# A two-layer cross-attention kernel: layer 0's context laid out with image rows first for every second entry, one value product shared by two entries, five semantic products for six, and a rewritten end

## The chip, the cores and the metric

The kernel runs on one core of a Trainium2 chip. The metric is the device time of one execution in microseconds (us); where several runs are given, their median counts. TensorE is called PE below (PEld is its weight load), VectorE DVE, ScalarE ACT, GpSimd POOL, and SP is the engine whose queue issues most of the DMAs.

## The reference, cut to what matters

Two cross-attention layers follow each other over 16 entries. An entry has 256 queries of 320 channels and a context of 256 rows of 512 channels; there are 20 heads of 16 channels. Layer 0 takes the first 77 context rows as text and the other 179 as image rows:

```python
q, k_text, v_text = hidden @ Wq, text @ Wk, text @ Wv
probs = softmax(q_h @ k_h.T * scale)                     # 77 text keys, by head
text_out = probs @ v_h
ip_k, ip_v = ip @ Wk_ip, ip @ Wv_ip                      # 179 image keys
scores = q_h @ ip_k_h.T * scale
text_probs = softmax(q @ k_text.T * scale)               # over all channels, not by head
sem = ((text_probs @ text) @ ip.T) * scale               # "semantic" scores, one for all heads
ip_probs = softmax(scores + 0.5 * sem) * spatial_mask
out = (text_out + ip_probs @ ip_v_h) @ Wout + bout + hidden
```

Layer 1 takes all but the last four context rows as text and the last four as image rows, normalises the attended text by its length for its semantic scores, and is otherwise alike. Only its last steps are touched by the change.

## The kernel before, in words

**Precision.** A float32 number is held as a high and a low part in the PE's rounded format, and a product of two such numbers is three matmuls (high by high, high by low, low by high): `prod`, L240. `halves` makes the two parts: ACT copies the high part (L165) and DVE or POOL subtracts it for the low part (L168). A product's third block of 64 output channels holds two terms in one matmul's 128 columns (`prod_m`, L250), which `evacuate` adds up (L259 to L262).

**Slots.** The work is written as 80 slots for layer 0 and 80 for layer 1. Slot k of layer 0 stands for one group of four heads of one entry, so five slots are an entry and ten a pair of entries. `slot0` writes, in this order: the maxima of group k+1 (`maxima0`, L753, a transpose whose result a DMA of ACT's queue puts into the stack of queries), half of the scores of k+2 (`score0`, L745; DVE takes their maxima in L746 and L747), half of the scores of k with keys on the partitions (`turned0`, L769; ACT takes the exponential in L772 and POOL multiplies by the semantic factor `rs` in L775), the attended values of k-1 (`attend0`, L804), the other halves, and the DMAs of the stacks of k+4 (`stacks0`). Between these, `fill` places whatever task is due: a table at the end gives each task's steps their slots, shifted by ten for each pair c. The PE's order is the written one; a scheduler orders DVE, ACT and SP; POOL's queue is worked in its order.

**Stacks.** For each group a stack `ks` of keys holds 48 key rows, 77 rows of the semantic factors M (the text part of them zero) and two rows that pick a maximum; `qs` is its partner. Keys and queries reach the stacks through DRAM (`kd`, `qd`). There are four stacks of each. In `score0` the keys are the moving operand, in `turned0` they are the weights, cut into two tiles of 128 rows.

**Values of layer 0.** The context of a pair lies in four tiles (`cta`, `ctb`), text first and image rows behind it. The values of an entry are made by `values0_` in three products of 128 context rows: rows 0 to 127 by the text weights (`wC`), rows 0 to 127 by the image weights (`wD`) and rows 128 to 255 by `wD`. ACT writes each to `vr`, scaled by a mask of rows. A pair so takes six products of twelve matmuls, 128x320 each. `attend0` takes for every head the three parts in turn. Column 16 of each head in `vr` holds the mask, written once at the start by `marks` (L334).

**Semantic scores.** `tokens0` makes M from the text rows and the image rows (77 columns of weights, 192 moving; POOL clears M's text part, L435). `semantic0` multiplies queries by text keys in six matmuls for each half (L667): three blocks of channels, high and low parts of the queries, each by the 156 columns of `kt`, which holds high and low parts of the keys. POOL copies the keys to `kt` (L385).

**The start.** `begin` is ordered by hand. SP issues loads and small DMAs back to back, among them the rows of `ks` that pick a maximum (`fields`, `ks<-mt`).

**The end.** Slots 158 and 159 hold the last groups of layer 1, slot 160 what is left of them. `attend1` adds to the values of k (L954) a product for k-1 (L964) whose operand DVE finishes in L943 from a PE product (L942) and POOL's rest (L933). Behind slot 160 the entry before the last is closed (`close1`: L1073, `split`, project L610 and L613, DVE L850, `out_dram<-xc`), and then the last one (`close_last`): its residual is loaded to `xc`, and it ends in L1121 with the product of the image probabilities by `output_values`, a matrix prepared in L1092 to L1105.

## Time and profile before

| what | value |
|---|---|
| three runs | 1497.43 us median (1495.08 to 1497.73) |
| the profiled execution's own time | 1499.52 us |
| its span (first to last instruction) | 1497.7 us |
| granted PE clock, mean | 0.984 |
| PE, POOL, DVE, ACT busy | 95%, 81%, 78%, 59% |
| PE in the chain that ended last | 73% of the span |

A row of the windows view gives, for a stretch of the span, each engine's busy time with its instructions, the granted PE clock, the share of time in which the DMA engines were busy, and GB/s. A row of a timeline gives start, duration, engine, line, operation, operands, shapes and count, and in brackets how long the engine was idle before it and on what. A row of groups ends in total and mean duration and the idle time before them. A row "X" of the chain gives start, duration and what the time was spent on. Line numbers are those of the kernel before; the rows of order of the kernel after have its own.

### The profile page before, as it was taken

To read this page: it belongs to the slowest core of one execution; us is meant where nothing else is said; L and a number is where in the kernel's file an instruction comes from. 1 tells how busy PE (TensorE), PEld (TensorE's weight loads), DVE (VectorE), ACT (ScalarE), POOL (GpSimd) and SP (SyncE) were. 2 spreads that over 40 slices of the span, in tenths; PEclk is the share of its full clock that TensorE was granted. 3 is DMA by queue.
4 is the path that set the end of the run, shared out by engine and by line. 5 is a ranking of instruction groups with operands and counts; after the bars stand their busy time and mean duration, and the time that the engine had idled before them with its cause. 6 is when DMAs were issued, how large, how long until landed. Compare 5 with 4: busy or idle time off the path is not lost.

```text
span 1497.7 us, 36123 instructions
## 1 busy us (share of the span) xinstructions
PE 1427.8 (95%) x12740; PEld 1155.6 (77%) x12740; DVE 1170.2 (78%) x2593; ACT 884.8 (59%) x1975; POOL 1215.2 (81%) x1304
## 2 busy tenths in 40 slices
PE   8789999999999899789999999999999999999997
PEld 8678888888888778577777777777777777777765
DVE  5467777777777787878887788778877887788785
ACT  5346565656565555556666666666666666666562
POOL 4259797979797977887698879887988798879786
PEclk9799999999999999999999999999999999999999
DMA  7767787778787776775434434443444344433411
GB/s 237 201 185 217 201 228 200 217 206 224 199 231 193 219 200 173 186 216 150 145 102 132 127 108 128 127 127 108 127 128 127 109 126 129 127 108 103 122 26 39
DMA packets 230986, 234.32 MB, mean 156 GB/s; under 512 B 39127, under 2 KB 200678, under 8 KB 230790
## 3 DMA queue, kind: packets, MB, share of 16 engines
q1 hardware_dynamic: 228598, 230.71, 55.4%
q8 instruction: 102, 1.67, 0.5%
q10 hardware_dynamic: 2208, 1.30, 0.4%
q14 instruction: 78, 0.64, 0.1%
HBM read 118.04 MB, written 77.04 MB: 130 GB/s over the span
## 4 chain that ended last, share of the span: by engine, by line
PE 73%; DVE 8%; DMA 6%; POOL 6%; issue 3%; ACT 3%; SPq 1%; ACTq 0%; DVEq 0%; POOLq 0%
PE X L942 15%; PE X L240 14%; PE P L804 6%; PE X L610 5%; PE P L954 5%; PE S L745 5%; PE P L964 4%; PE T L769 4%; PE T L894 3%; PE S L900 3%; PE X L613 2%; PE X L250 2%; PE X L579 2%; POOL P L775 2%; DVE mn L747 1%
## 5 line engine op out<-in xcount | busy, mean ns | idle before, releaser
L775 POOL TENSOR_TENSOR P<-P,rs 128x512 f32<-128x512 f32 x320 | 414.4, 1318 | 90.2 <-ACT P L772 89.3
L933 POOL TENSOR_TENSOR wt<-P,ctb 128x512 f32<-128x512 f32 x320 | 410.6, 1308 | 72.8 <-ACT ctb L932 72.8
L942 PE MATMUL X<-ctb,gm 128*128 128x512 f32 x1120 | 305.4, 402 | 5.8 <-DVE wt L943 5.7
L772 ACT ACTIVATE P<-T 128x512 f32<-128x512 f32 x320 | 175.4, 594 | 159.5 <-PE T L769 101.9
L943 DVE TENSOR_TENSOR wt<-X,wt 128x512 f32<-128x512 f32 x320 | 216.1, 680 | 42.7 <-PE X L942 36.4
L942 PEld LDWEIGHTS X<-ctb,gm 128*128 128x128 f32 x1120 | 195.3, 188 | 39.0 <-DVE wt L943 8.7
L914 ACT ACTIVATE P<-T 128x512 f32<-128x512 f32 x320 | 173.0, 593 | 76.2 <-PE T L894 73.3
L932 ACT ACTIVATE ctb<-P 128x512 fp32r<-128x512 f32 x320 | 186.7, 627 | 36.8 <-PE X L942 33.1
L902 DVE TENSOR_REDUCE mn<-S 128x4 fp32r<-128x1008 f32 x160 | 191.3, 1196 | 0.0
L747 DVE TENSOR_REDUCE mn<-S 128x4 fp32r<-128x716 f32 x160 | 142.2, 889 | 0.0
L804 PE MATMUL P<-P,vr 128*32 128x256 f32 x1920 | 127.4, 396 | 5.3 <-DVE tmp L821 2.0
L745 PE MATMUL S<-ks,qs 125*128 125x256 f32 x640 | 117.7, 307 | 4.9 <-DMA ks<-M 2.8
L745 PEld LDWEIGHTS S<-ks,qs 125*128 125x128 f32 x640 | 89.0, 195 | 40.1 <-issue 20.9
L1031 POOL TENSOR_TENSOR r<-u,rs 128x40 f32<-128x40 f32 (+2 forms) x17 | 108.7, 6394 | 3.9 <-DVE u L1028 3.9
L769 PE MATMUL T<-qs,ks 127*128 127x256 f32 x640 | 108.2, 292 | 0.4 <-DMA qs<-mt 0.4
L746 DVE TENSOR_REDUCE mn<-S 128x4 fp32r<-128x308 f32 x160 | 74.4, 465 | 31.2 <-PE S L745 30.8
L815 DVE STREAM_TRANSPOSE nt<-P 128x512 f32<-128x512 f32 x80 | 56.9, 711 | 51.8 <-PE P L804 51.3
L769 PEld LDWEIGHTS T<-qs,ks 127*128 127x128 f32 x640 | 92.1, 198 | 2.0 <-DMA qs<-mt 1.0
L804 PEld LDWEIGHTS P<-P,vr 128*32 128x32 f32 x1920 | 57.2, 112 | 47.0 <-issue 8.1
L954 PE MATMUL P<-P,v1t 128*32 128x256 f32 x1280 | 85.7, 385 | 0.0
L964 PE MATMUL P<-wt,zone 128*32 128x256 f32 x1280 | 85.1, 381 | 0.3 <-DVE wt L943 0.3
L610 PE MATMUL X<-ho,wF 128*128 128x256 f32 x512 | 74.3, 287 | 6.5 <-ACT mt L755 4.0
(297 smaller groups left out, 2974.5 us busy)
## 6 DMA issues: line engine op xcount, KB each, us to landing
qd<-q SPq DMA_DIRECT2D x96, 256.0 KB
qs<-tph SPq DMA_DIRECT2D x64, 320.0 KB
rawc<-in_cT_dram SPq DMA_DIRECT2D x60, 256.0 KB
qs<-qd SPq DMA_DIRECT2D x80, 192.0 KB
ks<-kd SPq DMA_DIRECT2D x80, 192.0 KB
ks<-kd SPq DMA_DIRECT2D x160, 96.0 KB
qs<-qd SPq DMA_DIRECT2D x160, 96.0 KB
kd<-kst SPq DMA_DIRECT2D x57, 256.0 KB
```

Of the source, the lines that this page charges most:

```text
L240: last = mm(out, lhs(a, k), rhs(b, k), start=i == 0, stop=i == len(terms) - 1)
L745: mm(sp[:, h], Q[: XROW + T0, h, t * 128 : (t + 1) * 128], K[: XROW + T0, h], start=True, stop=True)
L769: mm(st[p][:, j], K[:KS0, 2 * p + j, t * 128 : (t + 1) * 128], Q[:KS0, 2 * p + j], start=True, stop=True)
L772: exp = anchor(nc.scalar.activation(pt, st[p], AF.Exp, scale=SCALE))
L775: anchor(nc.gpsimd.tensor_mul(pt, pt, rs[:, t : t + 1].to_broadcast([128, 2, S])))
L804: mm(pv[32 * s : 32 * s + 32, o : o + S], v[:, vt, h : h + 32], P[k, s // 2][:, t, s % 2], start=vt < 2, stop=vt != 1,)
L902: anchor(nc.vector.tensor_reduce(maxes[k + 2][:, t], sp[:, :, :T1], axis=AX.X, op=ALU.max))
L914: anchor(nc.scalar.activation(P[k, u][:, t], st[u], AF.Exp, scale=SCALE))
L932: nc.scalar.activation(R[k, u][:, t], P[k, u][:, t], AF.Copy, scale=0.5)
L933: anchor(nc.gpsimd.tensor_sub(W[k, u][:, t], P[k, u][:, t], f(R[k, u][:, t])))
L942: mm(yp, gm[:, gb], R[k, u][:, kt], start=i == 0, stop=i == len(blocks[n]) - 1)
L943: nc.vector.tensor_mul(W[k, u][:, n], yp, W[k, u][:, n])
```

## The change

**Layout.** Context tiles get 51 zero columns ahead and are laid out, for each half, as text of both entries (2 x 77), image rows of the even entry (179), 26 zeros, image rows of the odd entry (179) and one more column. Cuts of 128 columns out of this are: 51 zeros and the even entry's text; the odd entry's text; and one that holds 51 image rows of the even entry, zeros and 51 of the odd one. Even entries now have image rows first (179) and text last, odd ones text first.

**Values.** `values0_` makes two products for an entry and a new task `vm` one for both: five products for a pair. `mark` writes the mask columns at each entry, and `attend0` takes the parts of even entries in another order.

```diff
-    def values0_(b):
-        for t, (w,), lo, sc in ((0, wv0, 0, tmask[:, 0:1]), (1, wvi0, 0, tmask[:, 1:2]), (2, wvi0, 128, 1.0)):
+    def value_rows(ct, at, w, *to):
+        vp = bank()[:, :320]
+        prod(vp, lambda s, k: side(ct[k], s, at, 128), lambda s, k: w(s, k), 4)
+        for V, t, sc in to:
+    def values0_(b):
+        ct, i = ct0[b // 2], b % 2
+        V = mark(b)
+        value_rows(ct, T0 if i else -MIX, wv0[0], (V, 0, masks(b)[0]))
+        yield
+        value_rows(ct, CI + (CG + MIX if i else 0), wvi0[0], (V, 2, 1.0))
+    def values_mixed(c):
+        to = [(vr[(b + 2) % 3], 1, masks(b)[1]) for b in (2 * c, 2 * c + 1)]
+        value_rows(ct0[c], CI + 128, wvi0[0], *to)
+    def mark(b):
+        V = vr[(b + 2) % 3]
+        for t, m in enumerate(masks(b)):
+            nc.gpsimd.tensor_copy(vcols(V, V0W)[:, t, :, 16], m.to_broadcast([128, H]))
...
-        task(("v0", 2 * c), shifted(n, -7, -5.4, -5), lambda b=2 * c: values0_(b), *k)
-        task(("v0", 2 * c + 1), shifted(n, -4, -3.8, -3.4), lambda b=2 * c + 1: values0_(b), *k)
+        task(("v0", 2 * c), shifted(n, -7, -5.4), lambda b=2 * c: values0_(b), *k)
+        task(("vm", c), shifted(n, -4.2), lambda c=c: values_mixed(c), *k)
+        task(("v0", 2 * c + 1), shifted(n, -3.8, -3.4), lambda b=2 * c + 1: values0_(b), ("vm", c))
```

The first place is the PE between the attended values of groups 43 and 44, in a pair in the middle of layer 0 (`wD` and `cta`, `ctb` are the image weights and the context, `vr` the values, `P` the probabilities). Before:

```order
L769 MATMUL T<-qs_95,ks_99 128x256 x4
L240 MATMUL X<-wD,cta_81 128x320 x3
L240 MATMUL X<-wD,cta_82 128x320 x3
L240 MATMUL X<-wD,ctb_83 128x320 x3
L240 MATMUL X<-wD,ctb_84 128x320 x3
L240 MATMUL X<-wD,cta_81 128x320 x3
L240 MATMUL X<-wD,cta_82 128x320 x3
L240 MATMUL X<-wD,ctb_83 128x320 x3
L240 MATMUL X<-wD,ctb_84 128x320 x3
L753 MATMUL X<-ident_r,mn_566 8x128 x2
```

The same place after (L252 is L240 before, L862 is L769, L846 is L753):

```order
L862 MATMUL T<-qs_95,ks_99 128x256 x4
L252 MATMUL X<-wD,cta_81 128x320 x3
L252 MATMUL X<-wD,cta_82 128x320 x3
L252 MATMUL X<-wD,ctb_83 128x320 x3
L252 MATMUL X<-wD,ctb_84 128x320 x3
L846 MATMUL X<-ident_r,mn_613 8x128 x2
```

One of two products of twelve matmuls is gone there; the other products of a pair stay in their slots, two of them in exchanged order.

**Copies that come in pieces.** The halves of the context and the evacuation of image keys are written in two pieces, text and image, or one for each entry. Key texts are 154 columns wide, not 156, and the copies to `kt` are 154 wide; the third block of keys is also copied to partitions 64 to 127.

```diff
             if i:
-                halves(*ahead.pop(0), eng, wait)
+                hi, lo, src = ahead.pop(0)
+                if isinstance(hi, list):
+                    for piece in zip(hi, lo, by_side(src)):
+                        halves(*piece, eng, "pieces")
...
-                    nc.gpsimd.tensor_copy(kt[:n, m, :, :, :T0], f(kst[:n, :, :, :T0]))
+                    for h in range(2):
+                        for p in range(0, 128, n):
+                            nc.gpsimd.tensor_copy(kt[p : p + n, m, h, :, :T0], f(texts(kst)[:n, h]))
```

The second place is POOL, in a pair in the middle of layer 0, from a group's last copy of attended values on (`hsn`). `cta` and `ctb` are the context's low parts, `P` the probabilities times `rs`. Before:

```order
L824 COPY hsn<-hsn 128x8x16
L435 MEMSET M_260 77x2x77
L775 TENSOR_TENSOR P_120<-P_120,rs_115 128x512
L775 TENSOR_TENSOR P_121<-P_121,rs_115 128x512
L168 TENSOR_TENSOR cta_81<-rawc_118,cta_81 128x512
L822 TENSOR_TENSOR hsn<-tmp_808 128x8x16
L168 TENSOR_TENSOR cta_82<-rawc_117,cta_82 128x512
```

After, where L868 is L775, L175 is L168 and L919 is L822:

```order
L868 TENSOR_TENSOR P_121<-P_121,rs_116 128x512
L868 TENSOR_TENSOR P_122<-P_122,rs_116 128x512
L175 TENSOR_TENSOR cta_81<-rawc_119,cta_81 128x154
L175 TENSOR_TENSOR cta_81<-rawc_119,cta_81 128x2x179
L175 TENSOR_TENSOR cta_82<-rawc_118,cta_82 128x154
L175 TENSOR_TENSOR cta_82<-rawc_118,cta_82 128x2x179
L919 TENSOR_TENSOR hsn<-tmp_848 128x8x16
```

The copy of `hsn` and the clearing of M are gone from POOL's queue, and each subtraction of 512 columns has become two.

**Semantic scores, M and the stacks.** The low parts of the third block of queries lie on partitions 64 to 127 of the same tile, so five matmuls do for six. M's zeros are written once at the start, at both ends of a wider tile. The stacks `ks` are 77 columns wider; even entries use them from column 77 on (`turned_ks`), and `fields` issues one more small DMA for each of the four.

```diff
-            for k in range(3):
-                qt = lambda h: qh[:, h, k, t * 128 : (t + 1) * 128]
-                for h in range(2):
-                    mm(sf[:, : 2 * NT].rearrange("p (s n) -> p s n", s=2), qt(h), kt[:, k], start=k + h == 0, stop=k + h == 3)
+            for k, h in ((0, 0), (0, 1), (1, 0), (1, 1), (2, 0)):
+                qt = qh[:, h, k, t * 128 : (t + 1) * 128]
+                mm(sf[:, : 2 * NT].rearrange("p (s n) -> p s n", s=2), qt, kt[:, k], start=k + h == 0, stop=k == 2)
...
-        Q, K = QK[k] = qs[k % SIZES["NR"]], ks[k % SIZES["NR"]]
+        Q, K = QK[k] = qs[k % SIZES["NR"]], (ks if b % 2 else turned_ks)[k % SIZES["NR"]]
...
             dma(ks[i][XROW + T0 : KS0, :, :T0], ind0r[:2, :T0].unsqueeze(1).to_broadcast([2, 4, T0]))
+            dma(ksw[i][XROW + T0 : KS0, 4 * S :], ind0r[:2, :T0])
```

**An entry's last group.** The sum of attended values is written by DVE to both places at once, in layer 0 (POOL's addition and copy, L822 and L824, go) and in layer 1 (POOL's copy L1014 goes).

```diff
-        nc.gpsimd.tensor_add(hn[:, g // 2, :, g % 2], tmp[:, 0], tmp[:, 1])
         if g == NG - 1:
-            nc.gpsimd.tensor_copy(hn[:, 2, :, 1], hn[:, 2, :, 0])
+            nc.vector.tensor_add(hn[:, 2], *[tmp[:, i].unsqueeze(2).to_broadcast([128, 8, 2, 16]) for i in range(2)])
             later(0.45, lambda: gather(0, b))
+        else:
+            nc.gpsimd.tensor_add(hn[:, g // 2, :, g % 2], tmp[:, 0], tmp[:, 1])
```

**The end.** From slot 155 on the maxima are taken one slot earlier. `output_values` gets earlier slots, the last entry loads its residual to a buffer of its own (`P`) and splits to `q`, no longer after the close of the entry before, and the last two subtractions of L933 are DVE's.

```diff
+LATE = 2 * NS - 5
...
-        if k > NS:
+        if NS < k <= LATE:
             yield lambda: maxima(k + 1)
...
+        if LATE <= k < 2 * NS:
+            yield lambda: maxima(k + 2)
...
+            eng = nc.vector if (k, u) == (2 * NS - 1, 1) else nc.gpsimd
+            anchor(eng.tensor_sub(W[k, u][:, t], P[k, u][:, t], f(R[k, u][:, t])))
...
-        y = load(x1d[b], "xc")
+        y = load(x1d[b], "P", bufs=SIZES["NP"])
         yield
-        hh = split(results["gathered", 1, b], tmask[:, 6:7], nc.vector, "ho")
+        hh = split(results["gathered", 1, b], tmask[:, 6:7], nc.vector, "ho", "q")
...
-    task(("ov",), [2 * NS - 3, 2 * NS - 2, 2 * NS + 0.6, 2 * NS + 1], output_values, ("o1", B - 1), ("w4", 1))
-    task(("c1", B - 1), [2 * NS + t for t in (4.5, 4.6, 4.7, 4.7, 4.7, 9)], close_last, ("c1", B - 2))
+    task(("ov",), [2 * NS - 4, 2 * NS - 3, 2 * NS - 1.4, 2 * NS - 0.7], output_values, ("o1", B - 1), ("w4", 1))
+    task(("c1", B - 1), [2 * NS + t for t in (0, 1.52, 1.61, 1.62, 1.63, 9)], close_last)
```

The third place is the PE behind the last group's values, at the kernel's end (`gm` is a Gram matrix of layer 1, `hq` and `wF` make the output values, `rs` the image values by probabilities). Before:

```order
L942 MATMUL X<-ctb_84,gm 128x512 x4
L1073 MATMUL X<-rs_115,rs_114 128x256 x3
L1092 MATMUL X<-ident,xq_91 128x128 x3
L942 MATMUL X<-ctb_84,gm 128x512 x3
L1101 MATMUL X<-wF_991,hq_230 128x320 x5
L1103 MATMUL X<-wF_991,hq_230 128x256
L1104 MATMUL X<-wF_991,hq_230 128x64
```

After (L1037 is L942, L1171 is L1073, L1059 is L964, L702 and L705 are L610 and L613, L1219 is L1121):

```order
L1037 MATMUL X<-ctb_84,gm 128x512 x4
L1171 MATMUL X<-rs_116,rs_115 128x256 x3
L1037 MATMUL X<-ctb_84,gm 128x512 x3
L1059 MATMUL P<-wt,zone 32x256 x8
L702 MATMUL X<-ho_193,wF_1041 128x256 x16
L705 MATMUL X<-ho_193,wF_1041 128x256 x5
L702 MATMUL X<-q_347,wF_1041 128x256 x16
L705 MATMUL X<-q_347,wF_1041 128x256 x5
L1219 MATMUL X<-rs_116,xq_91 128x256 x3
```

The transposes of L1092 and the products of L1101 to L1104 stand in slots 158 and 159 now, ahead of the last groups' values.

223 lines of the change are left out of this document (141 added, 82 removed).

## The prediction

> **What bounds the kernel now.** I read the page first: busy times, then the chain that ended last.
>
> ```profile
> PE 1427.8 (95%) x12740; PEld 1155.6 (77%) x12740; DVE 1170.2 (78%) x2593; ACT 884.8 (59%) x1975; POOL 1215.2 (81%) x1304
> PE 73%; DVE 8%; DMA 6%; POOL 6%; issue 3%; ACT 3%; SPq 1%; ACTq 0%; DVEq 0%; POOLq 0%
> ```
>
> PE is busy for 95% of the span and carries the chain. An average hides stages, so the windows come next: layer 0 in its even run, the end of layer 0, layer 1, and the last 65 us.
>
> ```profile
> 158.00:308.00 150.00, 147.11 (x1403) 127.39 (x1403) 115.80 (x273) 88.33 (x208) 131.67 (x128) 1.00 0.76 213
> 608.00:683.00 75.00, 64.36 (x595) 50.67 (x588) 57.11 (x124) 37.94 (x83) 65.85 (x74) 0.94 0.69 186
> 758.00:1433.00 675.00, 667.64 (x5952) 519.58 (x5944) 561.20 (x1193) 429.29 (x918) 566.86 (x620) 1.00 0.42 118
> 1433.00:1498.00 65.00, 53.99 (x445) 37.99 (x434) 43.65 (x95) 26.15 (x51) 49.34 (x54) 0.95 0.12 34
> ```
>
> PE sets the pace in layer 0 (147.11 of 150) and layer 1 (667.64 of 675), so a matmul taken out of either is worth its time, as long as POOL, at 131.67 of 150 in layer 0, keeps up. Where layer 0 ends and in the last 65 us PE waits for 11 us each; there chains count.
>
> Does POOL keep up? The next rows are four slots in which POOL splits the next context, and one whole pair of entries:
>
> ```profile
> 192.87:222.76 29.89, 29.51 (x285) 25.58 (x284) 24.04 (x57) 19.43 (x46) 29.83 (x30) 1.00 0.82 230
> 185.41:259.91 74.50, 73.30 (x702) 63.61 (x701) 57.94 (x136) 44.30 (x105) 65.72 (x64) 1.00 0.76 214
> ```
>
> A pair takes 74.5 us, of which POOL works 65.7; but in four of the ten slots (15 to 18) it works 29.83 of 29.89 us, without PE being held (29.51). POOL is the second bound.
>
> **The change part by part. Values.** This is the PE's timeline at the place shown in the change:
>
> ```profile
> 404.03 1.05 PE L240 MATMUL X<-wD,cta 128*128 128x320 f32 x6
> ...
> 406.68 1.04 PE L240 MATMUL X<-wD,ctb 128*128 128x320 f32 x6
> 407.56 0.28 PE L753 MATMUL X<-ident_r,mn 128*8 128x128 f32 x2
> 407.68 0.69 PE L745 MATMUL S<-ks,qs 125*128 125x256 f32 x4
> 408.20 0.64 PE L769 MATMUL T<-qs,ks 127*128 127x256 f32 x4
> 408.68 0.70 PE L240 MATMUL X<-cta 128*77 128x192 f32 x6
> 409.22 0.69 PE L240 MATMUL X<-ctb 128*77 128x192 f32 x6
> 409.84 1.50 PE L804 MATMUL P<-P,vr 128*32 128x256 f32 x24
> ```
>
> The four rows of six (two left out) lie at 0.88 us from each other. From start to start 24 matmuls take 407.56 - 404.03 = 3.53 us, 0.147 each; the twelve that go are 1.77 us. Eight pairs make 14.1. In six pairs I count it in full, 10.6; the last pair ends in the stage where PE waits anyway (64.36 of 75), so 0.7 of it, 1.2; the first lies in the start, where chains of DMAs count, so nothing: **-11.9 us** (-10.6 to -13).
>
> [...]
>
> **Semantic products and M.** Five for six is 192 to 160 matmuls of 156 columns.
>
> ```profile
> 398.45 1.46 PE L667 MATMUL X<-kb,q 128*128 128x156 f32 x12
> 399.75 0.28 PE L753 MATMUL X<-ident_r,mn 128*8 128x128 f32 x2
> L667 PEld LDWEIGHTS X<-kb,q 128*128 128x128 f32 x186 | 23.4, 191 | 5.1 <-DVE q L262 4.4 <-DVE xc L850 0.3 <-ACT q L259 0.2
> ```
>
> Twelve took 1.30 us, 108 ns each, so 32 are 3.5 us. Some start late for DVE's last part of q (4.4 us of waiting in the row of loads), and what is saved there turns into waiting: **-2.5** (-1.3 to -3.5). [...] M's products take 408.68 to 409.84, 97 ns for 192 columns; 180 save at most a sixteenth of it, 6 ns, over 192 matmuls 1.1: **-0.6** (0 to -1.1).
>
> **POOL in layer 0.** These groups price it; the last three are layer 1's, nearest in size to the new pieces:
>
> ```profile
> L168 POOL TENSOR_TENSOR cta<-rawc,cta 128x512 fp32r<-128x512 f32 x42 | 55.2, 1316 | 4.6 <-ACT cta L165 4.6
> L385 POOL CAST kb<-kst 128x308 fp32r<-128x308 f32 x14 | 6.2, 441 | 0.8 <-DVE rn L460 0.8
> L435 POOL MEMSET M<- 77x154 f32 x16 | 3.6, 226 | 21.2 <-PE X L697 21.0
> L822 POOL TENSOR_TENSOR hsn<-tmp 128x128 f32<-128x128 f32 x80 | 41.0, 513 | 5.6 <-DVE tmp L821 5.1 <-DVE mx L674 0.5
> L824 POOL COPY hsn<-hsn 128x128 f32<-128x128 f32 x16 | 4.8, 300 | 0.1
> L1007 POOL COPY tmp<-nt 128x48 f32<-128x48 f32 x80 | 18.3, 228 | 3.8 <-DVE nt L1000 3.8
> L1051 POOL TENSOR_TENSOR rs<-a,z 128x160 f32<-128x160 f32 x15 | 7.1, 470 | 0.9
> L1036 POOL TENSOR_TENSOR a<-a,si 128x160 f32<-128x160 f32 x15 | 8.1, 537 | 0.0
> L1064 POOL TENSOR_TENSOR rs<-rs,kb 128x384 f32<-128x384 f32 x15 | 17.8, 1185 | 1.1 <-DMA rs<-vipd 1.1
> ```
>
> A subtraction of 512 (1.316) becomes 154 and 358 columns. At the cheapest, 470 x 154/160 + 1316 x 358/512 = 1.37; at the dearest, 537 x 154/160 + 1185 x 358/384 = 1.62. I take +0.25 each (nearer the dear end, as 1185 is the row nearest to 358 columns), four times a pair: +1.0. The three casts of 308 columns become eight of 154; between 300 at 128 columns and 441 at 308 that is 0.32 each, 2.56 for 1.32: +1.24. Four mask copies of 20 columns a pair at about 0.21 (228 at 48 columns): +0.84. Gone are two memsets (-0.45) and at the two last groups an addition and a copy (2 x 0.81 = -1.63). Net **+1.0 on 65.7** a pair, while the pair shrinks to 72.6: 92%. In the full slots POOL gets about +1.0 from the context and loses 0.8. So PE is held there a little: I take 0.3 us a pair in seven pairs, **+2.0** (0 to 0.8 each, 5.6). POOL's wait for L697 (21.0) goes with the memset; PE was not held by it. Even entries' `attend0` reads the second half of `P` from the 9th of its 24 matmuls on, not from the 17th: a third of its 1.50 us, 0.5 us less for a late L775 product, which is part of the bound of 0.8.
>
> [...]
>
> DVE and ACT get more pieces too, but work 57.9 and 44.3 of 74.5 in the row of a pair; nothing.
>
> **The start.** SP issues without a gap, and the four `ks<-mt` have a row:
>
> ```profile
> 17.24 3.17 SPq L85 DMA_DIRECT2D ks<-mt  x4
> ```
>
> Four more are 3.17 us in front of everything that SP issues behind them; part is taken up where SP itself waits, and M's and the masks' work on POOL is gone from there: **+1.5** (0 to 3.2).
>
> **The end.** PE's last stretch before, with POOL's two powers and the chain's last steps:
>
> ```profile
> 1475.03 1.56 PE L1073 MATMUL X<-rs,rs 128*128 128x256 f32 x6 [1.61 <-DVE rs L1063]
> 1482.47 3.06 PE L610 MATMUL X<-ho,wF 128*128 128x256 f32 x16
> 1485.37 0.74 PE L613 MATMUL X<-ho,wF 128*128 128x256 f32 x5
> 1474.64 5.44 POOL L1031 TENSOR_TENSOR r<-u,rs 128x32 f32<-128x32 f32 x1
> 1484.22 1.65 POOL L1031 TENSOR_TENSOR r<-u,rs 128x8 f32<-128x8 f32 x1 [0.29 <-DVE u L1028]
> 1487.11 2.55 DMA out_dram<-xc
> 1489.68 3.25 DMA xc<-x1d
> 1493.02 1.27 DVE xc L1122 x3
> ```
>
> Before, the store of entry 14 (2.55) and the load of entry 15's residual into the same `xc` (3.25) follow each other before DVE may end (1493.02). With a buffer of its own that load is long done, and the last DVE step hangs on PE: the projection of entry 14 (L610 and L613) ran from 1482.47 to 1486.11, 3.65 us. Now ahead of it stand only the closing product and 3 matmuls of L942, so it begins about 3 us earlier, at 1479.4; entry 15's follows until 1486.7, L1121, as many matmuls as L1073's 1.56, until 1488.2, DVE's 1.27 and a last 0.4 overlap it in part, and it ends at 1489.3 instead of 1493.02 + 1.7 = 1494.7. POOL's chain (powers 5.44 and 1.65, then small steps in turn with DVE) must be through by 1486.7; its second power ended at 1485.9, and it starts some 2.5 us earlier, as two subtractions of 1.3 go to DVE, so 3.3 us are left for those steps: near a tie, and I add 0.5 for a late one. The products moved ahead (between L1073's row and L610's) now delay the last groups instead, where PE is full: 1.5 us back. Against that, 1479.4 is late for an engine whose wait of 1.61 is gone: PE may begin 1 to 2 us sooner, and I take 2. -5.4 + 0.5 + 1.5 - 2 is -5.4, rounded **-5.5** (-3 to -8). The loads that move with these steps are issued by SP in a stage with a DMA share of 0.12; nothing.
>
> **Sum**, against the profiled run of 1499.5 us: -11.9 - 2.5 - 0.6 + 2.0 + 1.5 - 5.5 = -17.0, which gives 1482.5. That run was 2.1 above the median of 1497.4; so the median comes to **1480.4**. Layer 1 between its ends keeps its matmuls and its time.
>
> **The rivals.** *POOL takes the bound.* If the full slots (29.83 of 29.89) set layer 0's pace, PE's earlier end only waits: the pair then gains about 0.6 instead of 1.77 - 0.3, the sum is about -11, the median 1487. For it speaks that row, against it that PE was not held in it (29.51). *The start and the end give little* (+3 and -2): -12, 1485.5. For it speaks that the end's POOL chain is nearly as long as PE's.
>
> *Slower: reads from odd places.* Even entries' keys now start at column 77 of `ks`, both as moving operand (L745) and as weights (L769): 16 matmuls in 40 slots, 640. From 27 ns each (17.0 / 640) the gain is gone. If each cost half of its distance more (four in 408.20 - 407.68, 130 ns, so 65), that is 42 us, and the median 1522. No row of before shows just this; the nearest shows cheap reads: key products start at column 76 with 360 columns and take 328 ns, against 312 for 320 from column 0.
>
> ```profile
> L240 PE MATMUL X<-cta,wB 128*128 128x360 f32 x96 | 18.5, 328 | 0.6 <-DVE sp L670 0.6
> L240 PE MATMUL X<-wD,cta 128*128 128x320 f32 x192 | 34.0, 312 | 0.1
> ```
>
> *The order's gain is eaten elsewhere*, by waits for maxima or for `vr` that the product at a new place brings to every pair: 0 in sum, 1497.
>
> **How the numbers follow.** My forecast 0.66, POOL 0.12, start and end 0.10, odd reads 0.08, eaten 0.04. All but the last two are faster: 0.88, same 0.04, slower 0.08; 0.2%, 3 us, is about what a measurement of this kernel can tell. The forecast's own terms reach from -10.6 - 1.3 + 5.6 + 3.2 - 3 = -6.1 to -13 - 3.5 - 1.1 - 8 = -25.6; against 1497.4 that is 1471.8 to 1491.3. The range is 1471 to 1491; it holds both faster rivals and leaves out the last two.
>
> **What would show it.** Right: pairs of layer 0 take 72.6 to 73.2 us, the block at L240 three quarters as long, POOL at 66 to 67 of it, S and T matmuls of even entries as long as those of odd ones, and the last 27 us some five shorter. Wrong: PE waiting for L775's products in every pair, S or T groups of even entries over 0.6 us from start to start, or an end that waits for POOL's powers.

## The result, and the profile after

The changed kernel is slower: 1517.42 us, the median of 6 runs (1507.65 to 1528.42), against 1498.07 for the kernel before (6 runs, 1495.08 to 1504.19); the ratio is 1.012, with an interval of 1.0072 to 1.0169. The prediction was 1480.4 us, faster. The profiled execution took 1528.42 us, the slowest of the six, with a span of 1526.7.

The page after, busy times and the chain that ended last:

```profile
PE 1436.2 (94%) x12612; PEld 1156.1 (76%) x12612; DVE 1228.5 (80%) x2643; ACT 887.6 (58%) x2031; POOL 1207.7 (79%) x1356
PE 59%; DVE 16%; POOL 10%; DMA 6%; issue 5%; ACT 2%; SPq 2%; ACTq 0%; DVEq 0%; POOLq 0%
```

PE has 128 matmuls fewer, exactly those that the change takes out, but is busy 8.4 us longer. DVE's share of the chain doubled from 8% to 16%, and DVE is busy 58 us longer with 50 instructions more. POOL, the engine that the prediction feared for, is busy 7.5 us less.

Cut at the attended values of fixed groups, the two profiled executions compare so (us; layer 1 begins with group 80):

| stretch | before | after | change |
|---|---|---|---|
| start to group 4 | 110.9 | 110.3 | -0.6 |
| five pairs, groups 4 to 54 | 373.9 | 390.2 | +16.3 |
| 54 to 80 | 211.7 | 213.4 | +1.7 |
| 80 to 84, the first slots of layer 1 | 40.7 | 45.5 | +4.8 |
| 84 to 154, 14 entries | 695.3 | 708.4 | +13.1 |
| 154 to the end | 65.1 | 58.9 | -6.2 |

That is +29.1 by these rounded figures; the spans differ by 29.0. The windows after, for a pair, for layer 1, and behind the last attended values:

```profile
188.49:266.72 78.23, 74.51 (x687) 63.32 (x685) 64.57 (x142) 44.38 (x112) 65.30 (x70) 0.96 0.75 203
863.00:1425.00 562.00, 550.03 (x4851) 427.11 (x4849) 471.38 (x968) 348.95 (x749) 460.24 (x496) 1.00 0.43 119
1505.70:1526.70 21.00, 15.29 (x117) 11.34 (x116) 15.67 (x39) 3.04 (x6) 12.20 (x17) 1.00 0.11 36
```

A pair that took 74.50 us at a granted clock of 1.00 takes 78.23 at 0.96. DVE's time in it went from 57.94 to 64.57 us for 6 instructions more. In layer 1 PE's share fell from 98.9% to 97.9%.

**One place in each pair of layer 0.** DVE's timeline at the split of an even entry's queries (L328 is L285 before, the third block, an operation with two operands in SBUF, `hq` and `xq`). First the same place before, DVE and then PE:

```profile
212.91 0.42 DVE L821 TENSOR_TENSOR tmp<-nt,P 128x256 f32<-128x256 f32 x1
213.25 0.81 DVE L285 SCALAR_TENSOR_TENSOR hq<-hq,tmask,xq 128x256 fp32r<-128x256 f32 x1
214.49 1.14 PE L240 MATMUL X<-cta,wB 128*128 128x360 f32 x6
```

And after, DVE:

```profile
293.90 0.17 DVE L912 TENSOR_TENSOR P<-P,mk 128x8 f32<-128x8 f32 x1
294.39 3.44 DVE L328 SCALAR_TENSOR_TENSOR hq<-hq,tmask,xq 128x256 fp32r<-128x256 f32 x1 [0.31 <-ACT hq L326]
297.75 0.41 DVE L914 TENSOR_TENSOR tmp<-nt,P 128x256 f32<-128x256 f32 x1
298.08 0.22 DVE L761 TENSOR_TENSOR sp<-sp,X 128x77 f32<-128x77 f32 x1
```

POOL at the same time:

```profile
291.06 5.01 POOL L868 TENSOR_TENSOR P<-P,rs 128x512 f32<-128x512 f32 x4
296.01 1.28 POOL L327 TENSOR_TENSOR hq<-xq,hq 128x512 fp32r<-128x512 f32 x1
297.22 0.33 POOL L465 CAST kb<-kst 128x154 fp32r<-128x154 f32 x1
298.24 0.46 POOL L919 TENSOR_TENSOR hsn<-tmp 128x128 f32<-128x128 f32 x1 [0.69 <-DVE tmp L914]
```

And PE, with the window around it:

```profile
295.04 0.64 PE L862 MATMUL T<-qs,ks 127*128 127x256 f32 x4
298.36 2.17 PE L252 MATMUL X<-cta,wB 128*128 128x360 f32 x6 [2.69 <-DVE sp L761]
300.32 2.00 PE L252 MATMUL X<-ctb,wB 128*128 128x360 f32 x6
290.04:302.26 12.22, 9.53 (x72) 8.18 (x72) 9.37 (x21) 5.10 (x15) 10.75 (x12) 0.82 0.76 204
```

L328 takes 0.48 us when nothing disturbs it. Here it takes 3.44, and ends 0.28 us behind the end (297.55) of POOL's run of multiplications, subtraction and cast. POOL stops there only because its next step needs DVE's L914, which stands behind L328. DVE's L761 stands there too, and PE waits 2.69 us for it; then six matmuls that took 1.14 us before take 2.17, and the granted clock of the stretch from 290 to 302 is 0.82. All five pairs have such an L328, of 3.33 to 3.50 us; before, the same step took 0.48 to 0.81, with the product of the attended values (L821 before, L914 after) ahead of it on DVE and not behind it. The group of these matmuls answers to the row of the prediction (18.5 us, 328 ns, 0.6 of waiting):

```profile
L252 PE MATMUL X<-cta,wB 128*128 128x360 f32 x96 | 23.0, 384 | 15.0 <-DVE sp L761 15.0
```

**One place in each entry of layer 1.** The same two steps, DVE and POOL, in the kernel before:

```profile
912.81 0.57 DVE L285 SCALAR_TENSOR_TENSOR hq<-hq,tmask,xq 128x256 fp32r<-128x256 f32 x1
912.57 0.53 POOL L1036 TENSOR_TENSOR a<-a,si 128x160 f32<-128x160 f32 x1
913.06 1.49 POOL L284 TENSOR_TENSOR hq<-xq,hq 128x512 fp32r<-128x512 f32 x1
```

And after:

```profile
937.00 1.58 DVE L328 SCALAR_TENSOR_TENSOR hq<-hq,tmask,xq 128x256 fp32r<-128x256 f32 x1
936.51 0.54 POOL L1133 TENSOR_TENSOR a<-a,si 128x160 f32<-128x160 f32 x1
937.00 1.30 POOL L327 TENSOR_TENSOR hq<-xq,hq 128x512 fp32r<-128x512 f32 x1
```

Before, DVE came first: it began 0.25 us ahead of POOL's subtraction, which was stretched to 1.49. After, both begin in the same 10 ns, POOL's takes its 1.30 and DVE's 1.58. One microsecond in each of eleven or twelve entries, and PE sees it as a wait for the maxima (L996) that stand behind it on DVE, which was not there before: 0.6 us of idle PE in an entry, half of what the entry loses. The waits of PE in layer 1:

```profile
PE S L994 <- DVE mn L996: 6.3, 11, 0.6
PE X L1037 <- DVE wt L1038: 5.5, 10, 0.6
```

**Which steps stretch.** Minimum, median and maximum (ns) of three DVE steps after; the third reads one operand from PSUM (`X`) and one from SBUF, the two others both from SBUF:

```profile
L328 DVE SCALAR_TENSOR_TENSOR hq<-hq,tmask,xq x32: 474/1562/3499, 12.6 to 1397.4; 128x256 fp32r<-128x256 f32 x32
L916 DVE TENSOR_TENSOR hsn<-tmp x16: 414/1180/2466, 115.4 to 713.7; 128x256 f32<-128x256 f32 x16
L1038 DVE TENSOR_TENSOR wt<-X,wt x320: 648/682/694, 721.8 to 1512.4; 128x512 f32<-128x512 f32 x160
```

None of L1038's 320 stretches, though POOL is busy for 460 of layer 1's 562 us. L916 is the sum that the change moved to DVE; its worst one is at the border of the layers, where PE then waits 1.30 us, again for L996:

```profile
713.73 2.47 DVE L916 TENSOR_TENSOR hsn<-tmp 128x256 f32<-128x256 f32 x1
717.77 0.80 PE L994 MATMUL S<-ks,qs 48*128 48x256 f32 x4 [1.30 <-DVE mn L996]
```

**The end** answers to the prediction's rows so, PE first, then POOL's powers:

```profile
1513.70 2.14 PE L702 MATMUL X<-ho,wF 128*128 128x256 f32 x16
1517.63 2.04 PE L702 MATMUL X<-q,wF 128*128 128x256 f32 x15 [0.83 <-DVE q L327]
1521.19 1.56 PE L1219 MATMUL X<-rs,xq 128*128 128x256 f32 x6 [0.93 <-DVE rs L1155]
1509.46 5.44 POOL L1128 TENSOR_TENSOR r<-u,rs 128x32 f32<-128x32 f32 x1 [0.33 <-DVE u L1125]
1516.08 1.65 POOL L1128 TENSOR_TENSOR r<-u,rs 128x8 f32<-128x8 f32 x1
```

The load between the two entries is gone from the chain, the last entry's projection follows the other's, and the closing product waits 0.93 us for the end of POOL's and DVE's chain: the near tie.

### The profile page after: what moved, and what is told of

Same layout as the page of the kernel before. It is cut to its first block, busy times and chain, and to the rows that moved or that the text cites. A ratio compares the mean times of both kernels' runs of the same rounds, so it can differ in the third digit from the quotient of the medians.

```text
span 1526.7 us, 36136 instructions
## 1 busy us (share of the span) xinstructions
PE 1436.2 (94%) x12612; PEld 1156.1 (76%) x12612; DVE 1228.5 (80%) x2643; ACT 887.6 (58%) x2031; POOL 1207.7 (79%) x1356
## 4 chain that ended last, share of the span: by engine, by line
PE 59%; DVE 16%; POOL 10%; DMA 6%; issue 5%; ACT 2%; SPq 2%; ACTq 0%; DVEq 0%; POOLq 0%
PE X L252 12%; PE X L1037 11%; PE P L897 6%; PE X L702 5%; PE S L837 4%; POOL wt L1028 4%; PE T L862 3%; PE P L1049 3%; DVE wt L1038 3%; PE P L1059 3%; POOL r L1128 3%; PE S L994 3%; PE T L988 2%; SPq L90 2%; DVE mn L840 2%
## 5 line engine op out<-in xcount | busy, mean ns | idle before, releaser
L868 POOL TENSOR_TENSOR P<-P,rs 128x512 f32<-128x512 f32 x320 | 413.7, 1315 | 126.3 <-ACT P L865 125.8
L1028 POOL TENSOR_TENSOR wt<-P,ctb 128x512 f32<-128x512 f32 x318 | 405.0, 1298 | 88.1 <-ACT ctb L1026 87.9
L1037 PE MATMUL X<-ctb,gm 128*128 128x512 f32 x1120 | 307.6, 403 | 6.3 <-DVE wt L1038 6.0
L1038 DVE TENSOR_TENSOR wt<-X,wt 128x512 f32<-128x512 f32 x320 | 216.2, 681 | 50.6 <-PE X L1037 46.9
L1037 PEld LDWEIGHTS X<-ctb,gm 128*128 128x128 f32 x1120 | 195.9, 189 | 40.5 <-DVE wt L1038 9.2
L996 DVE TENSOR_REDUCE mn<-S 128x4 fp32r<-128x1008 f32 x160 | 191.6, 1198 | 0.0
L837 PE MATMUL S<-ks,qs 125*128 125x256 f32 x640 | 120.1, 312 | 6.8 <-DMA ks<-kd 3.2
L837 PEld LDWEIGHTS S<-ks,qs 125*128 125x128 f32 x640 | 90.3, 197 | 42.5 <-issue 25.8
L1128 POOL TENSOR_TENSOR r<-u,rs 128x40 f32<-128x40 f32 (+2 forms) x17 | 108.7, 6396 | 3.4 <-DVE u L1125 3.3
L862 PE MATMUL T<-qs,ks 127*128 127x256 f32 x640 | 106.7, 289 | 1.1 <-ACT P L865 0.7
L839 DVE TENSOR_REDUCE mn<-S 128x4 fp32r<-128x308 f32 x160 | 74.4, 465 | 34.9 <-PE S L837 34.8
L862 PEld LDWEIGHTS T<-qs,ks 127*128 127x128 f32 x640 | 91.2, 196 | 2.7 <-ACT P L865 1.1
L272 ACT CAST kst<-X 128x179 fp32r<-128x179 f32 (+5 forms) x117 | 36.0, 329 | 83.5 <-PE X L252 49.0
L1059 PE MATMUL P<-wt,zone 128*32 128x256 f32 x1280 | 84.4, 379 | 0.0
L994 PE MATMUL S<-ks,qs 48*128 48x256 f32 x640 | 75.8, 314 | 8.5 <-DVE mn L996 8.2
```

The source lines that it names most:

```text
L837: mm(sp[:, h], Q[: XROW + T0, h, t * 128 : (t + 1) * 128], K[: XROW + T0, h], start=True, stop=True)
L862: mm(st[p][:, j], K[:KS0, 2 * p + j, t * 128 : (t + 1) * 128], Q[:KS0, 2 * p + j], start=True, stop=True)
L868: anchor(nc.gpsimd.tensor_mul(pt, pt, rs[:, t : t + 1].to_broadcast([128, 2, S])))
L996: anchor(nc.vector.tensor_reduce(maxes[k + 2][:, t], sp[:, :, :T1], axis=AX.X, op=ALU.max))
L1028: anchor(eng.tensor_sub(W[k, u][:, t], P[k, u][:, t], f(R[k, u][:, t])))
L1037: mm(yp, gm[:, gb], R[k, u][:, kt], start=i == 0, stop=i == len(blocks[n]) - 1)
```

## The experiments

The theory after the two traces: a DVE step with two operands in SBUF is held up where POOL multiplies, subtracts or casts without a pause (L328 took 3.44 us for 0.48, L916 2.47 for 0.41; L1038, with one operand in PSUM, never over 0.69), and the change put DVE's third block of the split, and its new sum, at such places. The rivals: POOL's own load; the copy taken out of layer 1; the new order on DVE, by which its queue is late whatever POOL does. Ratios are to the kernel before, run in the same group of runs (medians of 1499.95 to 1500.81).

**E1: the third block on POOL.** In splits on POOL, the third block is subtracted there, on partitions 64 to 127.

```diff
+        if tag == "hq" and eng is nc.gpsimd:
+            order(eng.tensor_sub(hl[64:, 2], src[64:, 2], f(hl[64:, 2])))
+            return hl
```

> The kernel after, but the third block of the query split (L328, tag hq) is made by POOL on partitions 64 to 127 instead of by DVE. Theory (DVE's step with two SBUF inputs stands still while POOL runs back to back): the 3.4 us stalls of layer 0 and the 1.6 us ones of layer 1 go, PE no longer waits 2.7 us a pair nor falls to a low clock; POOL gets about 0.6 us more per entry. Time 1478 to 1490. Rival (even entries' reads from odd columns, or POOL's own load, cost the time): no gain, or slower by POOL's extra 20 us of work, 1515 to 1535.

1504.15 us (10 runs), ratio 1.0019 (0.9992 to 1.0047). Pairs 75.55, 73.08, 75.06, 74.97 and 73.01; entries of layer 1 mostly 50.2. POOL has 31 instructions more:

```profile
L329 POOL TENSOR_TENSOR hq<-xq,hq 64x256 fp32r<-64x256 f32 x31 | 24.6, 792 | 2.4
```

24.6 us more on POOL, and the kernel is 13 us faster (by the ratios to before, 1.0019 against 1.012, 15): POOL's load is not what cost. The expected 1478 to 1490 was missed: pairs and entries recover, but the total is no better than that of the kernel before.

**E2 and E3: the copy of layer 1.** E2 puts layer 1's copy of `hsn` back on POOL in the kernel after; E3 takes it out of the kernel before.

```diff
         if g == NG - 1:
-            nc.vector.tensor_mul(hn[:, 2], wide(na[:, :, 0:16]), rz.unsqueeze(2).unsqueeze(3).to_broadcast([128, 8, 2, 16]))
+            nc.gpsimd.tensor_copy(hn[:, 2, :, 1], hn[:, 2, :, 0])
```

> The kernel after, with layer 1's last group of an entry settled as before (DVE multiplies into one place, POOL copies it to the other). Theory: the copy delays POOL's subtraction of the query split by 0.3 us, DVE's third-block step gets in ahead of it again (0.6 us instead of 1.6), an entry of layer 1 takes 50.0 us instead of 51.15; 15 entries, so about 16 us less than the kernel after: 1500. Layer 0 keeps its stalls. Rival (something else of the change slows layer 1): an entry stays at 51.1 us, time 1517.

> The kernel before with one part of the change alone: in layer 1 DVE writes the last group's result to both places and POOL's copy is gone. By count POOL loses 0.29 us of work an entry and DVE gains about 0.15; read so, nothing changes (1497). Theory: POOL's subtraction now starts ahead of DVE's third-block step, which takes 1.6 us instead of 0.6, and an entry takes 51.1 instead of 50.0 us: slower by about 16 us, 1514.

E2: 1517.89 us, 1.012 (1.0069 to 1.0171), entries still 51.12. E3: 1497.69, 0.9977 (0.9943 to 1.0011), entries still 49.97. Both expectations failed: the copy had nothing to do with it.

**E4: the odd entries' third block later in layer 0.** For odd entries DVE's third block is written 0.6 slots behind the rest of the split. The step that stalls is the even entries', which the edit does not touch; but the order around it changes: DVE has the product of the attended values ahead of it again, and POOL its sum `hsn` ahead of the subtraction, not behind it.

```diff
+        third = lambda: order(nc.vector.scalar_tensor_tensor(hl[:, 2], f(hl[:, 2]), neg, src[:, 2], op0=ALU.mult, op1=ALU.add))
+        later(slots, third) if slots else third()
...
+        xs = split(x, tmask[:, 5:6], nc.gpsimd, "hq", None, 0.6 if b > 1 and b % 2 else 0) if b else xs0.pop()
```

> The kernel after, with the third block of odd entries' query splits in layer 0 written 0.6 slots later, by which DVE's order is that of the kernel before at the place of the stall: the attended values' product (L914 of the kernel after) ahead of the third block. Theory: DVE's step then follows another without a gap and takes the first end of a POOL instruction (0.8 us instead of 3.4), PE does not wait, five pairs lose 4.5 to 5.5 us each: 1490 to 1497, layer 1 unchanged at 51.1 us an entry. Rival (POOL back to back blocks it wherever DVE asks): stalls stay, 1517.

1513.74 us (9 runs), 1.0096 (1.0065 to 1.0127). The even entries' step takes 0.48 us in all five pairs (the odd entries', at its new place, 0.46 to 1.44), and pairs take 76.67, 73.64, 73.71, 73.92 and 74.21: what the pairs lost is back, but for the first. Layer 1 keeps its 51.1 an entry, as it had to. The five pairs together take 372.1 us, against 390.2 in the profile of after and 382.8 in that of E14, the same kernel; yet in the medians E4 gains only 4 to 6 us on that kernel, and 9 on top of E5 (E8, below), and the expected 1490 to 1497 was missed. Part of it is given back between groups 54 and 84: E5's profile has 391.7 us in the five pairs and 247.8 there, E8's 371.5 and 256.3. Why is not known.

**E5: the third block of queries as before, in layer 1 only.** The evacuation puts the low parts beside the high ones (`beside`) in layer 0 alone; the DMA that reads them follows. PE, DVE, ACT and POOL keep the order of the kernel after.

```diff
-            evacuate(qh[:, 0, m], qh[:, 1, m], pp, m, beside=True)
+            evacuate(qh[:, 0, m], qh[:, 1, m], pp, m, beside=l == 0)
```

> The kernel after, but in layer 1 the low part of the third block of queries is written beside the second part as before (its own columns, partitions 0 to 63); layer 0 keeps the change. The trace of after has DVE's step of that evacuation 0.10 us later than before, and DVE 0.25 us later from there on, which lets POOL's subtraction in ahead of the third-block step. Theory: an entry of layer 1 takes 50.0 us again, 14 entries, 16 us less than after: 1501. Rival (the lateness comes from elsewhere): 51.1 us an entry, 1517.

1505.40 us, 1.0034 (1.001 to 1.0058): about 12 us less than the kernel after, from a line in another function. Entries take 49.9 to 50.0 again, and the third block in twelve of them:

```profile
L328 DVE SCALAR_TENSOR_TENSOR hq<-hq,tmask,xq x12: 576/606/635, 825.2 to 1374.5; 128x256 fp32r<-128x256 f32 x12
```

(1556/1586/1644 in the kernel after, 552/581/645 before). In layer 1 the `beside` form saves no matmul; it delays DVE by some 0.1 us at the evacuation, which grows to 0.25 where the split comes, and that lets POOL in first. Pairs stay at 77.4 to 79.4.

**E6, E6 with E5, and E7: the sum.** E6 gives layer 0's sum and copy back to POOL, which brings DVE's order at the split back to that of before. E7 is the moved sum alone, on the kernel before.

```diff
+        nc.gpsimd.tensor_add(hn[:, g // 2, :, g % 2], tmp[:, 0], tmp[:, 1])
         if g == NG - 1:
-            nc.vector.tensor_add(hn[:, 2], *[tmp[:, i].unsqueeze(2).to_broadcast([128, 8, 2, 16]) for i in range(2)])
+            nc.gpsimd.tensor_copy(hn[:, 2, :, 1], hn[:, 2, :, 0])
```

> The kernel after, with layer 0's last group of an entry summed and copied by POOL as before, not by DVE. This takes away DVE's new step with two SBUF inputs and also, by the scheduler, puts the attended values' product ahead of the third block again at the place of the 3.4 us stall. Theory: pairs of layer 0 take 73 to 74 us instead of 78.2, the first slots of layer 1 take 40.7 instead of 45.5, layer 1 stays at 51.1: 1490 to 1495. Rival (POOL, with 1.6 us more a pair, is the bound): pairs of 75 us or more, 1510.

> Both: layer 0's last group on POOL as before, layer 1's low part of the third block in its own columns. Theory: pairs of 73 to 74 us, entries of layer 1 of 50.0 us, the end 6 us shorter: 1476 to 1482, faster than before. Rival: the gains are eaten by waits of another kind, 1497.

> The kernel before with one part alone: layer 0's last group of an entry summed by DVE into both places. The scheduler leaves the order of the third block as it is here, so by the theory only the new step itself may stand: 16 steps of 0.45 to 2.5 us on DVE. 1495 to 1505. Rival (the DVE sum by itself makes the after kernel slow): 1515.

E6: 1540.64 us, 1.0268 (1.0229 to 1.0307); with E5 1522.92, 1.0163 (1.012 to 1.0206); E7: 1502.44, 1.0015 (0.9994 to 1.0037). Both expectations of E6 failed, by over 40 us. With the order of before, DVE's third block still took up to 3.89 us, pairs 79.7 to 81.8, and a wait of another kind was added; in its pairs:

```profile
PE X L702 <- ACT ho L326: 14.2, 5, 3.0
```

So the order of DVE's queue alone does not decide; and against the kernel after, POOL's two steps more in each entry cost some 20 us. With E5 the third block of four of the five pairs took no more than 0.70 us, and pairs still 77.9 to 81.2: that second wait is enough. E7's pairs are undisturbed (74.6), but the first slots of layer 1 take 44.4 us instead of 40.7, and E6's take 40.6: what these slots lose comes from the sum on DVE. In E7 the stretch ahead of them (54 to 80) is 3.6 us shorter, though, and from 54 to 84 its 252.5 us are the 252.4 of before; that the sum costs the whole kernel anything is not shown.

**E8, E9 and E11: both places freed.** E8 is E4 and E5 together. E9 adds POOL's sum and copy for the last entry alone. E11 is E8 with the mixed product made twice, once for each entry.

```diff
-        value_rows(ct0[c], CI + 128, wvi0[0], *to)
+        for one in to:
+            value_rows(ct0[c], CI + 128, wvi0[0], one)
```

> The kernel after with both cures, each at one place of the collision: layer 0's third block of odd entries 0.6 slots later (as in the run with the third block after the product), layer 1's low part in its own columns. Theory (DVE's steps with two SBUF inputs stand behind POOL; the rest of the change does what it says): pairs of 73 to 74 us, entries of layer 1 of 50.0, the end as in after: 1488 to 1494, faster than before by 0.5%. Rival (the cures only move the stall): 1500 or more.

> The same, and the sum of the last group of layer 0's last entry (one step of sixteen) goes back to POOL with its copy. In the trace of after this one DVE step took 2.47 us at the start of layer 1, and PE waited 1.3 us and ran at a low clock behind it. Theory: the first four slots of layer 1 take 40.7 us instead of 43 to 45: 3 us less than the run before it in this list, 1485 to 1491. Rival: no difference.

> The version with both cures, but the mixed product is made twice, once for each entry: six products of twelve matmuls a pair, as before the change. It measures what the shared product is worth where no stall hides it. Forecast: 1.77 us of PE a pair, six to seven pairs, 10.6 to 11.9 us more than the version with both cures; pairs of 75.4 instead of 73.7. Rival (POOL or DVE sets the pace of layer 0 by now): under 4 us.

E8: 1495.95 us (10 runs), 0.9976 (0.9946 to 1.0006), just outside the expected 1488 to 1494 and not faster than before beyond its interval. E9: 1495.91, 0.9978 (0.9941 to 1.0015); its first slots take 43.8 us, not less, because PE now waits 1.7 us for `q`: the expectation was missed, and it is not settled why E6 has this border for 40.6. E11: 1515.66, 1.0094 (1.0063 to 1.0125), which is 19.7 us more than E8 and not the 10.6 to 11.9 expected. In E11's profile the stall is back in the first pair, where the third block takes 6.58 us and the pair 81.87; the total therefore does not measure the mixed product. The fastest two pairs of E8, whose third blocks took at most 0.60 us at the place of the stall:

```profile
183.90:257.30 73.40, 71.93 (x685) 61.51 (x684) 62.30 (x142) 44.01 (x112) 65.07 (x71) 1.00 0.81 216
257.30:330.90 73.60, 72.13 (x686) 61.51 (x684) 62.43 (x142) 44.30 (x112) 65.48 (x70) 1.00 0.81 216
```

And two undisturbed pairs of E11:

```profile
267.00:342.40 75.40, 73.54 (x698) 63.18 (x697) 61.56 (x142) 44.46 (x112) 65.44 (x70) 1.00 0.79 211
342.40:417.40 75.00, 73.67 (x697) 63.27 (x696) 61.80 (x142) 44.63 (x113) 65.44 (x70) 1.00 0.78 213
```

12 matmuls are worth 75.2 - 73.5 = 1.7 us a pair; the prediction took 1.77. Between the medians of all five pairs (74.45 and 75.41) it is 1.0. The rest of the change, the semantic products' saving included, costs a pair 75.2 - 74.5 = 0.7.

**E10: the new end alone, on the kernel before.** Its core:

```diff
+LATE = 2 * NS - 5
...
-        y = load(x1d[b], "xc")
+        y = load(x1d[b], "P", bufs=SIZES["NP"])
-        hh = split(results["gathered", 1, b], tmask[:, 6:7], nc.vector, "ho")
+        hh = split(results["gathered", 1, b], tmask[:, 6:7], nc.vector, "ho", "q")
...
-        if k > NS:
+        if NS < k <= LATE:
...
+        if LATE <= k < 2 * NS:
+            yield lambda: maxima(k + 2)
```

> The kernel before with the change's end alone (maxima of the last slots earlier, output values earlier, own buffers for the last entry, the last two subtractions on DVE). The forecast's term for it was -5.5 us (-3 to -8). Expected 1492 to 1495, with the last slots 1.7 us longer and the rest behind them 7 to 8 us shorter. Rival (the end's gain in after came from something else): 1497 to 1500.

1494.31 us (10 runs against 31 of before), 0.9958 (0.993 to 0.9986): -6.3 us; forecast -5.5. The end behind the last attended values takes 20.94 us instead of 28.97, and the ten slots ahead of it 1.5 more, as the prediction had it. In this profile, whose layer 0 is that of the kernel before, the first pair stalls too: a third block of 3.43 us, a pair of 77.26. The stall is therefore not new with the change, only rarer without it.

**E12 and E13: POOL waits.** In the kernel after, POOL copies one column that DVE's third block has written, ahead of its own subtraction. POOL gets 31 instructions and a wait more; at the places of the stall DVE's order is that of the kernel after. The edit moves one thing besides: in the splits that DVE makes alone (`ho`) the third block now stands ahead of DVE's subtraction, where it takes 0.67 us instead of 1.24 in the median. E13 adds E5.

```diff
-        order(eng.tensor_sub(hl[:, 3:5], src[:, 0:2], f(hl[:, 0:2])))
         order(nc.vector.scalar_tensor_tensor(hl[:, 2], f(hl[:, 2]), neg, src[:, 2], op0=ALU.mult, op1=ALU.add))
+        before = [order(eng.tensor_copy(gap, f(hl[:, 2, :1])))] if eng is nc.gpsimd else []
+        last = order(eng.tensor_sub(hl[:, 3:5], src[:, 0:2], f(hl[:, 0:2])))
+        if before:
+            queued(last, *before)
```

> The kernel after, with a wait added to POOL and nothing taken away: ahead of its subtraction of the query split POOL copies one column that DVE's third-block step has written, so it stands still until DVE is through. DVE's order stays that of after (the third block ahead of the attended values' product). Theory (DVE gets in when POOL pauses): the step takes at most 2.1 us instead of 3.4 in layer 0 (the rest of two products of POOL) and 0.6 instead of 1.6 in layer 1; pairs of 74 to 76 us, entries of 50.0 to 50.4; 1500 to 1505, faster than after in spite of the wait. Rival (DVE's step is slow for another reason, its own operands or a semaphore): POOL waits too, 1520 or more.

> The same wait, and layer 1's low part of the third block in its own columns. If the wait cures layer 1 by itself, this adds nothing: 1500 to 1505; if the wait holds POOL back there, entries of layer 1 are nearer 50.0 here: 1495 to 1500.

**E14: the kernel after again**, in the same group of runs, for its spread and a second profile.

> The kernel after, unchanged, on the same chip as the two above. Its first profile was of the slowest of six executions (1528 us, median 1517). Theory: layer 1 is as slow in every execution (51.1 us an entry), and what differs is how many of layer 0's third-block steps stand for three POOL instructions: pairs between 74 and 79 us. Rival: all five pairs take 78 us again.

E12: 1499.03 us (10 runs), 0.9993 (0.9969 to 1.0016). E13: 1493.59, 0.9963 (0.9941 to 0.9985); both came within 2 us of the range expected. E14: 1520.08 (4 runs, 1515.9 to 1525.49), 1.0137 (1.0097 to 1.0176). With one wait more on POOL (and the new order in DVE's own splits) the kernel is 21 us faster. The shorter `ho` step is unlikely to be what gives the time back, since entries take 49.95 with 1.51 us there in E5 and before; no run separates it. In E12 the place of the stall looks like this, DVE and then POOL:

```profile
219.94 2.02 DVE L328 SCALAR_TENSOR_TENSOR hq<-hq,tmask,xq 128x256 fp32r<-128x256 f32 x1 [0.38 <-ACT hq L327]
216.68 5.00 POOL L872 TENSOR_TENSOR P<-P,rs 128x512 f32<-128x512 f32 x4
222.09 0.19 POOL L329 COPY gap<-hq 128x1 f32<-128x1 f32 x1 [0.41 <-DVE hq L328]
```

DVE now ends behind the multiplications, since POOL stops there; it no longer stands through subtraction and cast. Pairs take 74.4 to 75.1, and entries 50.1. In layer 1 the step is undisturbed:

```profile
L328 DVE SCALAR_TENSOR_TENSOR hq<-hq,tmask,xq x12: 475/477/477, 821.5 to 1372.9; 128x256 fp32r<-128x256 f32 x12
```

E14's profile (1515.9 us) has pairs of 77.94, 73.46, 77.86, 77.22 and 76.27: the second pair of the very same kernel escaped. Its window and the next one's:

```profile
188.30:261.70 73.40, 72.11 (x685) 61.48 (x684) 61.22 (x142) 44.62 (x112) 65.57 (x71) 1.00 0.80 218
261.70:339.60 77.90, 73.37 (x690) 62.48 (x688) 64.89 (x142) 44.45 (x112) 65.28 (x70) 0.98 0.75 204
```

In the escaped pair L328 takes its 0.48 us, in the next one 3.50. So some 4 us of a pair come with this one step, and whether it stalls can differ within an execution; that alone can move an execution by 4 us a pair, which fits the kernel's wide spread.

## Why the prediction was wrong

**The step that failed** is one sentence: "DVE and ACT get more pieces too, but work 57.9 and 44.3 of 74.5 in the row of a pair; nothing." It priced DVE by its busy share. The runs showed that two DVE steps with two operands in SBUF, the third block and the moved sum, have no price of their own: in the kernel after the first cost 0.48 us or, where POOL worked without a pause, up to 3.50, the second 0.41 to 2.47, with everything queued behind them on DVE. The trace of before showed it already: its row of `hq` at L285 runs from 0.48 to 1.62 us, and its third block of `ho` takes 1.50 to 1.53 in 21 of 32 entries, where it began during a POOL instruction and ended 0.28 us behind that one's end. A look at the spread of each DVE group, and at what POOL does in the long ones, would have found the stretch; the prediction read only POOL's means and DVE's shares.

**A second, smaller miss in the same place:** the sum moved from POOL to DVE was counted as relief for POOL only (-0.81 twice), and the evacuation `beside` at nothing. The first makes the first slots of layer 1 about 4 us longer (E7, which has them back in the stretch ahead), the second costs layer 1 about 12 us (E5).

**Terms that held.** The mixed product: 1.7 us a pair where nothing disturbs it (E8 against E11), forecast 1.77. The end: -6.3 (E10), forecast -5.5. Undisturbed pairs come to 73.4 to 73.6 (E8, E14) instead of 72.6 to 73.2: the 0.7 that E11 leaves is more than the 0.3 for POOL with the semantic products' saving against it; its parts were not measured apart. POOL's own work was to grow by 1.0 us a pair from 65.7; in the undisturbed pairs it is 65.1 to 65.6, so that sum had the wrong sign. The start: forecast +1.5, the first 110 us are 0.6 shorter; as the same stretch takes 107.0 to 111.3 in the profiles that have the old start, that is nothing.

**The block at L240** was to be three quarters as long. At the place shown it is half as long, 12 matmuls for 24, which is what the working said and the last paragraph did not:

```profile
198.93 1.04 PE L252 MATMUL X<-wD,cta 128*128 128x320 f32 x6
199.81 1.05 PE L252 MATMUL X<-wD,ctb 128*128 128x320 f32 x6
```

**The rivals.** Reads from odd places cost nothing: from start to start, in the five pairs, the score matmuls of even entries take 150 ns in the median and of odd ones 152, the turned ones 120 and 119. That rival's 1522 is the forecast nearest to the result, by luck: its mechanism is not there. POOL as the bound came near in kind, since it is POOL's unbroken run that decides (in E12, where POOL stops, L328 took 2.02 us and not 3.44); but its own time is not what is missing (E1 and E12 give it more work and are faster). Layer 1 was said to keep "its matmuls and its time": it kept the matmuls and lost 13 us.

**What made it large.** The wait of PE behind a stalled DVE step is 2.7 us in a pair, and the pair loses 4.8 against the undisturbed one. The rest is the clock: PE works 74.51 us for the matmuls that take 72.11 in E14's undisturbed pair, at 0.96 against 1.00. At the place shown above the granted clock was 1.00 in the 8 us ahead of the wait of 2.69 us, with 0.42 us of idle PE in them, and 0.50 in the 3.9 us behind it:

```profile
287.67:295.67 8.00, 7.58 (x75) 6.39 (x73) 7.10 (x17) 4.67 (x13) 8.00 (x10) 1.00 0.80 223
298.36:302.26 3.90, 3.90 (x12) 3.50 (x13) 1.89 (x7) 1.78 (x5) 3.12 (x4) 0.50 0.68 151
```

What the clock follows was not tested apart.

**Shown and not shown.** Shown: the stalled step's place, and that taking it off DVE (E1), another order around it (E4, layer 0), letting DVE come first (E5, layer 1) or making POOL wait (E12) each gives back what its place lost. E5 is the cleanest of them, since the order of PE, DVE, ACT and POOL does not differ there. Not shown: what the two engines hold each other up by. The traces give the kind of step that stretches on DVE (L328 at 474 to 3499 ns and L916 at 414 to 2466, both operands in SBUF, against L1038 at 648 to 694, one in PSUM) and POOL's work beside it: at the place above, multiplications, a subtraction and a cast (3.44 us for 0.48). Not every POOL instruction does this: during the last 1.84 us of POOL's power of 5.44 us, whose two operands are in SBUF as well, DVE's two steps with two operands in SBUF take their undisturbed time:

```profile
1513.06 0.69 DVE L327 TENSOR_TENSOR ho<-hT,ho 128x512 fp32r<-128x512 f32 x1
1513.67 0.48 DVE L328 SCALAR_TENSOR_TENSOR ho<-ho,tmask,hT 128x256 fp32r<-128x256 f32 x1
```

**Open:** why DVE gets in at the end of the first POOL instruction in some cases (0.81 us at 213.25 before, where the same multiplications run) and only at POOL's pause in others. The order on DVE goes a long way: over the even entries' third blocks in the five pairs of all traces that have them on DVE, those that began more than 0.2 us ahead of the end of a POOL multiplication got in at that end in 17 of 24 cases with the attended values' product directly ahead of them on DVE, and in none of 28 with the product behind. It does not decide alone (four of E6's five stall with the product ahead), nor does the time to POOL's end, which is 0.21 to 0.53 us where DVE got in and 0.26 to 0.74 where it did not. Those that began within 0.2 us of the end all got in. Open too is the border of the layers in E9, and why E4 gains less in its median than its pairs show.

No version beat the kernel before by more than its new end does: E13 (0.9963) and E10 (0.9958) agree within their intervals. The layout with five value products brings about 1 us a pair where nothing disturbs it, and gives it back in the pairs that stall and between groups 54 and 84 (259.3 us in E13, 252.4 before).

## What to carry to other kernels

Before moving a step to an engine "with room", list its operands: on DVE, a step with two SBUF operands beside a POOL that multiplies, subtracts or casts without a pause can cost several times its length (3.50 us for 0.48 here), and all that is queued behind it waits too (PE by 2.69 us); the spread between minimum and maximum of each DVE group in the trace of before shows where this already happens (481 to 1617 ns for L285). Where it does, a wait added to the other engine can be the cheapest cure (21 us here with one copy of one column an entry, E12). In these traces the step got in more often where it stood directly behind another DVE step (17 of 24 against none of 28); no run tests that alone. A change in one stage (`beside`, for layer 0) should not be applied to another that gains nothing by it: 0.25 us of delay there turned the order of two engines around in every entry.

## What the runs showed of the hardware

- DVE's third block of 0.48 us took 3.33 to 3.50 us beside four POOL instructions, of which three had ended before it did (L328 in all five pairs of the kernel after; 3.50 in E14, and 6.58 in one pair of E11). The one that began at 294.39 ended 0.28 us behind the end of the fourth, a cast: it had not got in at the first of these ends.
- A POOL power of 5.44 us (L1128) held back neither of two such DVE steps in its last 1.84 us: L327 took 0.69 us, L328 0.48.
- POOL's subtraction took 1.49 us where DVE's step had begun 0.25 us ahead of it (L284 at 913.06 before), and 1.30 where both began together (L327 at 937.00 after).
- The granted PE clock was 0.82 over the 12.22 us from 290.04 after, with a single wait of 2.69 us in them.
- Reads that start at column 77 took PE no longer: in the five pairs after, 150 ns from start to start against 152 as moving operand (L837), 120 against 119 as weights (L862).
